# A fused five-stage kernel: inverse norms from Ln and Exp with a Newton step, band masks from half arrays, a new order of the local attention loop

## The chip, the cores and the metric

The kernel runs on one core of a Trainium2 chip. A core has five engines that run side by side, each with a queue of its own that it works off in order: TensorE (PE, matrix products into PSUM, with weight loads listed as PEld), VectorE (DVE), ScalarE (ACT), GpSimd (POOL[...]) and SyncE (SP, which here issues the transfers). Engines wait for each other by semaphores. The metric is the device time of one execution in microseconds, as the median of some runs.

## The reference

The model has two layers of attention and feed-forward on 4 sequences of 512 tokens of width 128: a gated convolution with a scan, a mixture of experts, a global attention, and last a six-layer local attention transformer. The change lies in that last part, which is most of the time. For each layer and head (16 heads of 64):

```python
def l2norm(t):
    return t / jnp.maximum(jnp.linalg.norm(t, axis=-1, keepdims=True), 1e-12)
...
qkv = x @ Wqkv
q, k, v = jnp.split(qkv, 3, -1)
...
q = l2norm(q) * qs
k = l2norm(k) * ksc
...
q = q * cos * scale + rotate_half(q) * sin * scale
k = k * cos * inv + rotate_half(k) * sin * inv
out = local_attention(q, k, v)
...
return out @ Wo
```

`local_attention` cuts the sequence into windows of 32 queries. A window sees its own 32 keys and the 32 before them, under a band mask, with scores multiplied by 8 and a softmax. After the attention comes a feed-forward with a layer norm and an exact GELU.

## The kernel before

The residual lies transposed (features on partitions) in SBUF. The local stage is cut into chunks of 128 tokens: 6 layers x 4 sequences x 4 chunks = 96 chunks, each an object of the class `Chunk`. What one chunk does:

- `query_up(j)` (L1159) makes 512 columns of queries (j = 0, 1) or keys (j = 2, 3) in PSUM. `square(j)` (ACT, L1166) and `squares(j)` (DVE, L1195) give the squared norms of the heads, `rotate_parts(j)` (DVE, L1178 and L1182) the two products of the rotation, which `rotate_sum(j)` (POOL, L1192) adds.
- `least_norms(j)` (DVE, L1203) clamps 16 squared norms from below, and `invert_norms(j)` (POOL, L1209) raises them to the power -1/2. That is done once for the keys (`rk`) and once for the queries (`rn`). `scale` (POOL, L1221) multiplies the keys by `rk`. The queries aren't multiplied: their `rn` enters as the scale of the softmax's exponential.
- `turn_up(j)` transposes on PE (L210), and `turn_down(j)` copies the result out of PSUM (L846), on ACT or DVE as the table `COPIES` says.
- `mask` (L1291) writes the band mask into the two PSUM banks of the scores: for each half of the heads one bf16 product of the identity with a 128 x 512 table. `scores(g)` (L1303) adds 128 small products, 64 rows by 32 columns of the array each.
- `largest` (DVE, L1315), `bias` (DVE, L1321) and `exponentials(g)` (ACT, L1331, 4 heads a call) make the softmax, `invert` (DVE, L1339) and `divide` (POOL, L1343) its division. `flip_up`/`flip_down` transpose the weights, `weigh` (L1379) multiplies them with the values, `lift` copies out, `output` (L1403) projects, and `add` (DVE, L1411) adds to the residual.
- `value`/`keep` (L1237, ACT L1243) make the values, and `spread` (SP, L1252 to L1257) copies them into the layout of the windows by 8 or 10 transfers a chunk.

The loop is a software pipeline. In turn i the tuple `TURN` is run through: an entry `(lag, step, ...)` runs that step of chunk i - lag. So a chunk's queries are made in one turn (lag 0), its scores in the next (lag 1), its softmax in the one after (lag 2), and so on to lag 4. The order in the tuple is the order in which each engine gets its instructions, and no engine departs from it. Turns with k = 1, 2 and 3 also take in the feed-forward of a finished sequence, a generator (`feedforward`) of which `advance` runs the next piece at the positions that `FEED` names: transposes and statistics, normalise (L202), transposes, gates with Gelu (L1431, L1436), three products (L1442), and the last product (L1452).

PSUM has two banks each for products (`mm`: query, value, projection and feed-forward products in turn) and for transposes (`tr`), and one pair each for the scores (`S`) and the weighed values (`o`). A product can start only when the bank used two products before has been read out.

The lists `MIDDLE` and `LAST` give the order by hand where the loop is filled from the global attention and where it is emptied into the last feed-forwards.

## Time and profile before

| | |
|---|---|
| Median of 3 runs | 2099.04 us (2096.14 to 2101.76) |
| The profiled execution | 2115.05 us, its span 2113.2 us |
| Mean granted TensorE clock | 0.985 |
| Global attention ends, local stage begins | at about 440 us |
| Rotation sums on POOL, L1192 | 384 x 1.275 us |
| Key scaling on POOL, L1221 | 192 x 1.043 us |
| Division on POOL, L1343 | 192 x 1.045 us |
| Exponentials on ACT, L1331 | 1536 x 0.435 us, each with a read of its sum, 0.235 us |
| Squares on ACT, L1166 | 384 x 0.633 us |
| PSUM copies 128x512, L846 | 0.59 to 0.65 us on ACT, 0.68 us on DVE |
| Normalise on DVE, L202 in the feed-forward | 88, of 0.291 at the least, 1.077 at the median |

Durations of neighbouring instructions of one engine overlap a little in the records; where a rate matters, the distance from start to start is the better measure. The profiled execution is one execution, and it took longer than the runs' median.

### The profile page before, as it was taken

Reading aid. Unit: us, or ns where it says so; the run is one execution under the profiler, and the core shown is the slowest. Engines: PE = TensorE matmul, PEld = TensorE weight load, DVE = VectorE, ACT = ScalarE, POOL = GpSimd, SP = SyncE. Lnnn points to the kernel's source line nnn. Section 1 sums busy time; section 2 is a strip of 40 time slices with the busy share of each in tenths; the row PEclk is TensorE's granted clock in tenths of the full one; section 3 lists DMA queues with packets and bytes.
Section 4 is the critical chain, followed back from the end, with each engine's and each line's share of the span. In section 5 each row is a group of like instructions: output and inputs, shape, how many; then the busy total and the mean of one; then the engine's idle time right before and its main releaser. Section 6 shows DMA issues by size and latency. Waiting matters only on the chain.

```text
span 2113.2 us, 80381 instructions
## 1 busy us (share of the span) xinstructions
PE 1980.1 (94%) x32980; PEld 1393.4 (66%) x32980; DVE 1615.3 (76%) x3343; ACT 1490.9 (71%) x4875; POOL 1722.8 (82%) x1388
## 2 busy tenths in 40 slices
PE   6778999999999999999999999999999999999997
PEld 4766777766566666666666666666666666666666
DVE  6447776687788887788877888778888788788874
ACT  2434344457788787888887788877887788877774
POOL 3425665589998899888999899998998999988882
PEclk9899999999999999999999999999999999999999
DMA  7530000002322224222232222232222322222221
GB/s 246 135 107 6 5 5 1 1 19 62 109 62 61 61 68 119 58 62 63 60 113 58 62 70 69 79 90 62 60 68 63 105 69 67 60 60 62 65 65 52
DMA packets 96665, 143.14 MB, mean 68 GB/s; under 512 B 17358, under 2 KB 41548, under 8 KB 95404
## 3 DMA queue, kind: packets, MB, share of 16 engines
q1 hardware_dynamic: 90828, 133.02, 23.3%
q8 instruction: 262, 4.29, 0.9%
q0 software_dynamic: 1472, 3.02, 0.7%
q10 hardware_dynamic: 4000, 1.97, 0.3%
q14 instruction: 103, 0.84, 0.1%
HBM read 36.36 MB, written 4.06 MB: 19 GB/s over the span
## 4 chain that ended last, share of the span: by engine, by line
PE 58%; DVE 14%; ACT 10%; issue 4%; DMA 3%; POOL 3%; SPq 2%; another core or an unknown queue 0%; ACTq 0%; DVEq 0%; POOLq 0%
PE q L1159 10%; PE lv L1237 6%; ACT lp L1331 6%; PE lo L1379 6%; PE ly L1403 5%; PE tp_r L210 5%; DMA vk<-vr 3%; PE ls L1303 3%; PE fa L1442 3%; PE fy L1452 3%; PE fg L1431 3%; PE gy L1028 2%; DVE lt L1182 2%; PE lpt L1356 2%; DVE fn L202 2%
## 5 line engine op out<-in xcount | busy, mean ns | idle before, releaser
L1331 ACT ACTIVATE lp<-ls,lnb,rn 128x64 f32<-128x64 f32 x1536 | 608.1, 435 | 32.2 <-DVE lnb L1321 31.9
L1192 POOL TENSOR_TENSOR ro<-lt,lt 128x512 f32<-128x512 f32 x384 | 484.4, 1275 | 54.2 <-DVE lt L1182 42.3
L1159 PE MATMUL q<-wqkvo,sA 128*128 128x512 f32 x768 | 383.2, 600 | 6.9 <-DVE sA L1411 4.4
L1178 DVE TENSOR_TENSOR lt<-q,rot 128x512 f32<-128x512 f32 x384 | 262.8, 684 | 148.6 <-ACT sq L1166 136.0
L1331 ACT ACTIVATION_READ_ACCUMULATOR lp<-ls,lnb,rn 128x1 f32 x1536 | 360.3, 235 | 0.0
L1209 POOL TENSOR_TENSOR rk<-rk,neg_half 128x16 f32<-128x16 f32 x96 | 279.0, 2906 | 52.3 <-DVE rk L1203 52.2
L1209 POOL TENSOR_TENSOR rn<-rn,neg_half 128x16 f32<-128x16 f32 x96 | 277.9, 2895 | 24.5 <-DVE rn L1203 22.0
L1166 ACT ACTIVATE sq<-q 128x512 f32<-128x512 f32 x384 | 235.3, 633 | 48.1 <-PE q L1159 28.7
L210 PEld LDWEIGHTS tp_r<-ident,ro 128*128 128x128 f32 x1536 | 183.6, 141 | 118.3 <-issue 94.5
L1182 DVE TENSOR_TENSOR lt<-q,rot 128x512 f32<-128x512 f32 x384 | 260.8, 679 | 0.0
L1195 DVE TENSOR_REDUCE ss<-sq 128x8 f32<-128x512 f32 x384 | 251.2, 674 | 2.3 <-ACT sq L1166 2.2
L1237 PE MATMUL lv<-wqkvo,sA 128*128 128x512 f32 x384 | 210.3, 630 | 23.2 <-DVE lt L1182 20.6
L1379 PE MATMUL lo<-lpT,vk 64*64 64x32 f32 x12288 | 206.0, 220 | 20.8 <-issue 19.6
L1243 ACT COPY vr<-lv 128x512 f32<-128x512 f32 x192 | 118.6, 618 | 151.2 <-PE lv L1237 98.7
L1379 PEld LDWEIGHTS lo<-lpT,vk 64*64 64x64 f32 x12288 | 192.3, 135 | 39.9 <-issue 37.9
L210 PE MATMUL tp_r<-ident,ro 128*128 128x128 f32 x1536 | 216.7, 274 | 1.6 <-ACT lpT L846 0.7
L1343 POOL TENSOR_TENSOR lp<-lp,lsum 128x512 f32<-128x512 f32 x192 | 196.5, 1045 | 9.7 <-DVE lsum L1339 9.7
L1221 POOL TENSOR_TENSOR ro<-ro,rk 128x512 f32<-128x512 f32 x192 | 196.2, 1043 | 7.4
L1159 PEld LDWEIGHTS q<-wqkvo,sA 128*128 128x128 f32 x768 | 128.7, 191 | 107.7 <-issue 45.4
L1403 PEld LDWEIGHTS ly<-oT,wqkvo 128*128 128x128 f32 x1536 | 182.2, 193 | 11.4 <-issue 10.6
L1403 PE MATMUL ly<-oT,wqkvo 128*128 128x128 f32 x1536 | 188.9, 277 | 0.3 <-ACT oT L846 0.3
L1303 PEld LDWEIGHTS ls<-kT,qT 64*32 64x32 f32 x12288 | 141.0, 105 | 43.4 <-issue 20.6
(305 smaller groups left out, 3628.8 us busy)
## 6 DMA issues: line engine op xcount, KB each, us to landing
vk<-vr SPq DMA_DIRECT2D x576, 128.0 KB
vk<-vr SPq DMA_DIRECT2D x336, 64.0 KB
wqkvo<-in_lwqkv_dram SPq DMA_DIRECT2D x6, 1536.0 KB
w<-in_ew_dram SPq DMA_DIRECT2D x20, 322.0 KB
wqkvo<-in_lwo_dram SPq DMA_DIRECT2D x6, 512.0 KB
ew<-in_ew_dram SPq DMA_DIRECT2D x8, 322.0 KB
ew<-in_ew_dram SPq DMA_DIRECT2D x8, 256.0 KB
lw<-in_lw_dram SPq DMA_DIRECT2D x6, 341.0 KB
```

What stands on the lines that cost most here:

```text
L210: nc.tensor.transpose(tp[:, c * P : (c + 1) * P], i[:, c, :], ident)
L1159: nc.tensor.matmul(q, lhsT=self.xs, rhs=self.w["qkv"][:, j * 512 : (j + 1) * 512], start=True, stop=True,)
L1166: nc.scalar.activation(self.sq[j], self.q[j], AF.Square)
L1178: nc.vector.tensor_tensor(heads(t1), heads(q), cs[:, None, :].to_broadcast([P, 8, DH]), ALU.mult)
L1182: nc.vector.tensor_tensor(swapped(t2), swapped(q)[:, :, ::-1, :], sn[:, None].to_broadcast([P, 8, 2, 32]), ALU.mult,)
L1192: nc.gpsimd.tensor_tensor(self.rot[j], *self.parts.pop(j), ALU.add)
L1195: nc.vector.tensor_reduce(self.ss[:, j * 8 : j * 8 + 8], heads(self.sq[j]), AX.X, ALU.add)
L1209: nc.gpsimd.tensor_tensor(self.r[j], self.r[j], neg_half.to_broadcast([P, HEADS]), ALU.pow)
L1237: nc.tensor.matmul(v, lhsT=self.xs, rhs=self.w["qkv"][:, (4 + j) * 512 : (5 + j) * 512], start=True, stop=True,)
L1331: nc.scalar.activation(self.P[:, i, :], self.S[:, i % 2, i // 2 * KB : (i // 2 + 1) * KB], AF.Exp, bias=self.nb[:, i : i + 1], scale=self. ...
L1379: nc.tensor.matmul(self.o[to : to + DH, odd, t0 : t0 + QB], lhsT=vk[r][lo : lo + KB, s, :], rhs=self.pT[lo : lo + KB, s, r * QB : (r + 1) ...
L1403: nc.tensor.matmul(y, lhsT=self.w["o"][:, j, :], rhs=self.oT[:, j % 2, j // 2, :], start=j == 0, stop=j == INNER // P - 1,)
```

## The change

It has four parts. The inverse norm is no longer a power on POOL. One clamp on DVE takes all 32 squared norms (queries and keys) and multiplies them by -1/2. ACT takes Ln and Exp of that for a first value y, and POOL makes one Newton step on y in four operations. At the start of the global attention and after each Gelu, the table set that holds both Ln and Exp is loaded ahead. `bias` goes from DVE to POOL. The band mask is no longer a product over 128 rows: the masks repeat every 32 queries, so 64 rows hold all that is needed, and the two products of a chunk use the upper and the lower 64 rows of the array, with a table `row_of` in place of the identity. Last, `TURN`, `COPIES` and `FEED` are new, with steps split finer. `MIDDLE` no longer holds three steps (`ru0.2`, `di1.0`, `ru3.2`), which now fall into the loop, and `LAST` begins with four steps more (`roa0 li0.0 di1.1 roa3`), since the loop hands over in another state.

```diff
+LOG_EXP = "natural_log_exp_and_others"
...
-NM = 2 * M_BAND + T
+NM = 2 * M_BAND + T + P
...
+    three_halves = cp.tile([P, 1], F32, name="three_halves")
+    nc.vector.memset(three_halves, 1.5)
...
+    row_of = mask_h[:, 2 * M_BAND + T :]
...
         def least_norms(self, j):
 
-            name = ("rn", "rk")[j]
-            self.r[j] = sm.tile([P, HEADS], F32, tag=name, name=f"{name}{self.tag}")
-            nc.vector.tensor_tensor(
-                self.r[j], self.ss[:, j * HEADS : (j + 1) * HEADS],
-                least.to_broadcast([P, HEADS]), ALU.max,
-            )
+            self.half_least(slice(j * HEADS, (j + 1) * HEADS), "nk"[j])
+            self.r[j] = self.x
+
+        def half_least(self, at, name):
+            x = sm.tile([P, 2 * HEADS], F32, tag="rn", name=f"r{name}{self.tag}")
+            self.x = x[:, 0 : at.stop - at.start]
+            nc.vector.tensor_scalar(self.x, self.ss[:, at], least, -0.5, ALU.max, ALU.mult)
 
         def invert_norms(self, j):
-            nc.gpsimd.tensor_tensor(
-                self.r[j], self.r[j], neg_half.to_broadcast([P, HEADS]), ALU.pow
-            )
...
+            self.inverse_root(self.r[j], "nk"[j])
+
+        def inverse_root(self, x, name):
+
+            n = x.shape[1]
+            y = sm.tile([P, 2 * HEADS], F32, tag="yn", name=f"y{name}{self.tag}", bufs=2)[:, 0:n]
+            nc.scalar.activation(y, x, AF.Ln, scale=-2.0)
+            nc.scalar.activation(y, y, AF.Exp, scale=-0.5)
+            nc.gpsimd.tensor_tensor(x, x, y, ALU.mult)
+            nc.gpsimd.tensor_tensor(x, x, y, ALU.mult)
+            nc.gpsimd.tensor_tensor(x, x, three_halves.to_broadcast([P, n]), ALU.add)
+            nc.gpsimd.tensor_tensor(x, x, y, ALU.mult)
+
+        def all_norms(self):
+
+            self.half_least(slice(0, 2 * HEADS), "qk")
+            self.r = [self.x[:, 0:HEADS], self.x[:, HEADS:]]
+
+        def invert_all(self):
+            self.inverse_root(self.x, "qk")
...
             for par in range(2):
+
+                at = slice(par * 64, par * 64 + 64)
                 nc.tensor.matmul(
-                    S[:, par], lhsT=ident_h, rhs=bands[min(self.c, 1)], start=True, stop=False
+                    S[:, par], lhsT=row_of[at], rhs=bands[min(self.c, 1)][at], start=True,
+                    stop=False,
                 )
...
+        nc.scalar.preload_act_table_set(LOG_EXP)
         yield
         for k, (f0, fn) in enumerate(DI_CH):
...
     TURN = (
-        (1, "squares", 3), (1, "rotate", 1), (1, "window"), (3, "flip", 0, "e6"),
-        (1, "values", 0), (2, "largest"), (1, "scale_keys"), (2, "bias", nc.vector),
-        (3, "flip", 1, "e7"), (2, "exponentials", 0), (1, "squares", 1), (4, "project"),
-        (2, "exponentials", 3), (1, "turn", 0, "e4"), (0, "query", 2), (1, "scale_queries"),
-        (0, "query", 0), (0, "rotate", 2), (0, "rotate", 0), (2, "exponentials", 2),
-        (1, "turn", 1, "e5"), (0, "squares", 2), (3, "weigh", 0), (3, "weigh", 1),
-        (2, "exponentials", 1), (2, "values", 1), (0, "query", 3), (1, "turn", 3, "e3"),
-        (0, "squares", 0), (1, "turn", 2, "e2"), (2, "invert", 1), (0, "query", 1),
-        (1, "mask"), (3, "lift", 1, "e1"), (2, "invert", 0), (1, "scores", 1),
-        (2, "divide", 0), (1, "scores", 0), (3, "lift", 0, "e0"), (2, "spread"),
-        (2, "divide", 1), (0, "rotate", 3),
+        (1, "rotate_sum", 0), (1, "rotate_parts", 1), (4, "lift", 0, "e0"), (3, "divide", 1),
+        (2, "largest"), (2, "bias", nc.gpsimd), (1, "rotate_sum", 1), (1, "value", 0),
+        (1, "squares", 3), (1, "keep", 0), (1, "rotate_sum", 3), (3, "flip_up", 0),
+        (3, "flip_down", 0, "e6"), (3, "flip_up", 1), (1, "window"), (1, "squares", 1),
+        (2, "exponentials", 0), (4, "output"), (4, "add"), (2, "exponentials", 1),
+        (1, "turn_up", 1), (0, "query_up", 2), (1, "turn_down", 1, "e5"), (0, "square", 2),
+        (1, "all_norms"), (3, "flip_down", 1, "e7"), (1, "invert_all"), (0, "rotate_parts", 2),
+        (0, "squares", 2), (0, "query_up", 0), (1, "scale"), (0, "square", 0),
+        (2, "exponentials", 3), (3, "weigh", 0), (3, "weigh", 1), (0, "rotate_parts", 0),
+        (2, "invert", 0), (2, "exponentials", 2), (1, "turn_up", 0), (1, "turn_down", 0, "e4"),
+        (3, "lift", 1, "e1"), (2, "value", 1), (1, "turn_up", 3), (0, "query_up", 3),
+        (0, "squares", 0), (2, "keep", 1), (2, "invert", 1), (0, "square", 3), (2, "divide", 0),
+        (1, "turn_down", 3, "e3"), (1, "turn_up", 2), (2, "spread"), (1, "mask"),
+        (0, "rotate_sum", 2), (0, "query_up", 1), (1, "turn_down", 2, "e2"), (1, "scores", 1),
+        (1, "scores", 0), (0, "rotate_parts", 3), (0, "square", 1),
     )
     COPIES = {
         "e0": "aaaa",
-        "e1": "avaa",
-        "e2": "aaaa",
-        "e3": "aaaa",
-        "e4": "avva",
-        "e5": "aavv",
-        "e6": "aavv",
-        "e7": "vavv",
+        "e1": "vavv",
+        "e2": "vvav",
+        "e3": "aava",
+        "e4": "vvaa",
+        "e5": "vvvv",
+        "e6": "vavv",
+        "e7": "vvvv",
     }
-    FEED = {1: (12, 36, 40), 2: (5, 12, 13), 3: (3, 11)}
+    FEED = {1: (7, 45, 55), 2: (10, 13, 20), 3: (17, 28)}
...
+        if i == 0:
+            nc.scalar.preload_act_table_set(LOG_EXP)
...
+    first[64:] = first[:64]
+    k, to = np.arange(P)[:, None] % 64, np.arange(P)[None, :]
+    row_of = np.where(to < QB, k == to, k == QB + to % QB)
+    m = np.concatenate([np.tile(first, (1, 8)), np.tile(band, (1, 8)), causal, row_of], 1)
```

## The prediction

> **What bounds the kernel now.** I read the page's busy shares first, then PE's timeline over one group of four chunks (a batch row of one layer), then busy time by engine over its four turns, then rows by shape. The page:
>
> ```profile
> PE 1980.1 (94%) x32980; PEld 1393.4 (66%) x32980; DVE 1615.3 (76%) x3343; ACT 1490.9 (71%) x4875; POOL 1722.8 (82%) x1388
> ```
>
> PE and POOL are both nearly full. A share can't say which one makes the others wait; the stretch by turns can (start:end, length, then busy time of each engine, the granted clock, DMA). I cut turns from one mask matmul to the next:
>
> ```profile
> 1215.32:1229.34 14.02, 14.02 (x311) 10.14 (x310) 10.16 (x21) 12.44 (x46) 13.79 (x10) 1.00 0.27 70
> 1229.34:1244.69 15.35, 14.70 (x315) 10.51 (x314) 14.20 (x33) 13.64 (x47) 15.27 (x13) 1.00 0.30 74
> 1244.69:1264.95 20.26, 19.19 (x325) 12.14 (x324) 17.38 (x31) 16.32 (x48) 17.25 (x14) 1.00 0.22 56
> 1264.95:1282.24 17.29, 17.29 (x319) 11.45 (x318) 14.45 (x27) 12.27 (x44) 15.07 (x12) 1.00 0.24 59
> ```
>
> In the first and last turn PE never stops: 14.02 us is its work for one chunk, the rest is the feed-forward laid into the turns. It loses time in the second, where POOL (fifth busy figure, 15.27 of 15.35) is full, and the third. PE's timeline there (start, duration, instruction, what it waited for):
>
> ```profile
> 1238.21 2.07 PE L1379 MATMUL lo<-lpT,vk 64*64 64x32 f32 x128
> 1240.83 1.10 PE L1237 MATMUL lv<-wqkvo,sA 128*128 128x512 f32 x2 [0.55 <-ACT lp L1331]
> 1242.03 1.10 PE L1159 MATMUL q<-wqkvo,sA 128*128 128x512 f32 x2
> ...
> 1246.70 0.55 PE L210 MATMUL tp_fb<-ident,fn 128*128 128x128 f32 x3
> 1247.88 0.33 PE L210 MATMUL tp_fb<-ident,fn 128*128 128x128 f32 x1 [0.64 <-DVE fn L202]
> 1248.05 0.60 PE L1356 MATMUL lpt<-ident,lp 128*128 128x128 f32 x4
> 1249.08 1.12 PE L1237 MATMUL lv<-wqkvo,sA 128*128 128x512 f32 x2 [0.43 <-DVE lt L1182]
> ```
>
> PE waits for DVE: for the feed-forward's normalise, and for a PSUM bank that the rotation parts empty. DVE is late because of POOL:
>
> ```profile
> 1233.03 1.13 DVE L1203 TENSOR_TENSOR rk<-ss,least 128x16 f32<-128x16 f32 x1
> 1243.76 4.07 DVE L202 TENSOR_SCALAR fn<-fn,mv_f,rs_f 128x128 f32<-128x128 f32 x4
> ```
>
> The first has a minimum of 0.155 and here takes 1.13, ending when POOL's two ro sums end (1234.1). A normalise takes 0.29 at best, 1.08 at the median, about one POOL instruction. Work of PE alone over the group: 14.02 + 14.46 (one more set of transposes, 0.44) + 18.9 (0.44 + 2.57 + 1.87 of feed-forward) + 17.29 = 64.7. Mask to mask the four turns average 67.8 over the stage (66.9 here). So PE loses 3.1 per group, and over 22 groups with a feed-forward in the table **about 68 us is the most that order and relief can give**, while PE's work stays.
>
> **The change, part by part.**
>
> *Powers on POOL.* Removed each turn:
>
> ```profile
> L1209 POOL TENSOR_TENSOR rk<-rk,neg_half 128x16 f32<-128x16 f32 x96 | 279.0, 2906 | 52.3 <-DVE rk L1203 52.2
> L1209 POOL TENSOR_TENSOR rn<-rn,neg_half 128x16 f32<-128x16 f32 x96 | 277.9, 2895 | 24.5 <-DVE rn L1203 22.0
> ```
>
> 5.80 us a turn. Added: four POOL operations on 128x32 and the bias on 128x16. POOL products on 128, 256 and 512 columns take 0.40, 0.62 and 1.04, so 1.67 ns a column on 0.18: 0.24 for 32 columns, 0.26 with some room for two full inputs (1.275 against 1.04 at 512), 0.21 for the bias. Together 1.25. POOL falls by 4.55 a turn, from 61.4 to 43 us in the group above. It ceases to bind.
>
> *Ln and Exp on ACT.* Nearest rows: 128x19 copy 0.18, 128x1 activation 0.20, 128x128 Exp 0.31. I take 0.23 each (ends 0.18 and 0.35) and 0.5 for both with the step between them. ACT loses 10 PSUM copies per group (22 "a" letters become 12) at 0.535 from start to start: 54.7 - 5.4 + 2.0 = 51 us.
>
> *Table loads.* Now a pair per feed-forward:
>
> ```profile
> L1436 ACT ACT_TABLE_LOAD x22 | 28.2, 1283 | 0.4
> L1331 ACT ACT_TABLE_LOAD x22 | 28.2, 1283 | 0.4
> ```
>
> The Trainium skill, "ScalarE: Activation LUTs", section "Table sets: the hidden batching unit", says that functions load as sets, that Exp lives in more than one, and that one set holds both Ln and Exp. The preload names that set after each Gelu, so the pair stays a pair: cost nothing. Were Ln and Exp taken from different sets, each turn would have two loads, 2 x 1.28 by the row or 2 x 2.66 by the page (which adds a drain): 2.6 to 5.3 us on ACT's busiest stretch in all 96 turns. I take nothing, and keep this as a rival.
>
> *DVE.* Ten copies come over at 0.60 from start to start, +6.0 a group; two clamps and the bias (means 0.40, 0.39, 0.26) become one clamp, -2.4. DVE goes from 56.2 to 60 us a group: the fullest engine behind PE. Cover is 4.7 us per group, not spread evenly.
>
> *Masks.* Now two 128-row bf16 products take, with the step into the scores' small tiles, 0.53 (1229.34 to 1229.87). Entering small tiles costs 0.10 (transposes 0.53 before the weighing, 0.44 before a projection), leaving them 0.10 (the value product takes 0.97 after the weighing and 0.86 elsewhere), so a mask is 0.21. On separate halves of the array the two run side by side, saving 0.21; that such halves overlap is seen in the scores, 128 products of 64 columns in 1.7 us where 64 columns at the projection's rate (0.86 per 512) would be 0.107 each, 13.7 in a row. But the masks now stand ahead of the second query product, no longer next to the scores. The Trainium skill, "TensorEngine Tiling (Array Packing)", section "Key Properties", says that changing the tiling mode drains the engine. That speaks against this part: one more entry and exit, +0.20. By the packing alone 96 turns gain 20 us; with the switches at the trace's price they gain 1. If the halves don't overlap they lose 19. I take zero.
>
> *The order table.* The chain of a turn, t = 0 at the end of the scores: maxima 0.1 to 1.3 on DVE; bias on POOL to 1.75 (before, the clamp stood between and was held until POOL finished: 1233.03 to 1234.59, 1.56, now 0.45); keep and eight exponentials (0.385 each) to 4.95; square 2 to 5.5; Ln and Exp to 6.1; four POOL steps to 7.3; key scaling 2 x 1.04 to 9.5; then transpose 3. PE without waits is at that transpose at 9.2 (value product 0.92, two flips 0.88, projection 1.79, a transpose 0.44, two query products 1.72, weighing with its entry 2.09, a transpose with the exit 0.53, value product 0.86). It waits 0.3, and the scores end near 14.3, against 14.02 before. Queued behind Ln on ACT are a square and the eight other exponentials; these end at 9.9, before the mask needs the bank at about 10.9. With a feed-forward: turn two has the normalise before the key copy on DVE. DVE gets there at 10.75 (maxima to 1.3, statistics 1.6, two reductions 1.2, add 0.6, copies 1.2, clamp 0.2, two rotation pairs 2.4, two reductions 1.2, the rest copies and a wait for the projection), POOL still has one division product and two sums; four normalises take 2.5 to 3.4, scores end at 16.3 to 16.75 (PE's own work 14.9 in this cut, with both transposes). Turn three: Gelus and loads to 5.9, exponentials, Ln at 9.8, scaling done 13.5, PE there at 13.5: 18.3. Turn four: scaling done 10.2, PE at 13: 17.5. Sum 66.4 to 66.85. Taking 66.8, **the group gains 1.0 of its 67.8**, 22 us over 22 groups. Value spreads keep their 8 or 10 transfers a chunk, 0.55 issue each; they start when the second value copy ends, 3.6 us before the turn's end (3.9 before), so SP's queue gains nothing and can cost 0.3. The lists before and after the loop move a few steps and shorten a few powers: zero.
>
> Sum: profiled span 2113.2, in an execution of 2115.1, minus 22 is 2091 and 2093. The runs' median lies 16 lower, 2099.0; minus 22 is **2077 us**.
>
> **Rivals.**
>
> *The new chain is longer than I walked (slower).* Place: the run from maxima to transpose 3, which has 0.3 us too much in turn one and nothing spare in turn three, and PE does nothing else meanwhile since its queue is in order. Each extra us costs up to two per group. It decides from 0.5 us extra, which hops or a clamp held by POOL (1.13 above) can give; with 1.2 extra the group loses 2.4 - 1.0 = 1.4, 31 us: 2130. For it: DVE, in this chain at both ends, gets fuller. Against: the 1.1 us saved ahead of the bias.
>
> *PE back to back.* If POOL, freed of a third of its work, no longer holds DVE's normalise (0.29 each, 3 us less), nearly all of the 3.1 comes back: 2099 - 63 = 2036. For it: the turns one and four of today. Against: DVE's added copies.
>
> *A wash.* Half-array masks cost their switches and the gain of turns two and three goes into turn one: 2096.
>
> *It doesn't do what it says.* Loads in every turn: 2.6 more in each chain, some 1.8 of it unhidden, 96 x 1.8: 2270.
>
> **How the numbers follow.** Main case 0.42, longer chain 0.24, back to back 0.19, wash 0.11, loads 0.04. Below 0.3% (6 us), a measurement here can't tell a change from none. Faster: 0.37 of the main case and all of back to back, 0.56 with rounding; within 0.3%: 0.05 + 0.09 + 0.02 = 0.16; slower: the rest, 0.28. The range 2028 to 2132 holds the two outer cases and leaves the loads and a worse chain out; the main case's own is 2062 to 2095.
>
> **What would show it.** Right: no powers of 2.9 us in POOL's rows; POOL near 65% of a turn; Ln and Exp at 0.2 to 0.25; 44 paired loads; normalise's mean well below 0.88. Chain: PE idle before transpose 3, released by POOL's scaling. Masks: 0.3 us from mask to query, the projection behind it 0.1 longer. Wrong: a turn without feed-forward over 14.8 us, PE waiting on DVE in every turn, or more than some 50 loads.

## The result, and the profile after

The changed kernel takes **2134.2 us** (median of 4 runs, 2125.4 to 2135.16), beside 2098.1 us (2096.14 to 2101.76) for the kernel before: a ratio of 1.0163 [1.0143, 1.0182]. It is slower by 1.6%; 2077 us and a gain were forecast.

The page of after, its head and the busy time of each engine:

```profile
span 2133.0 us, 80093 instructions
PE 1986.8 (93%) x32980; PEld 1365.6 (64%) x32980; DVE 1689.1 (79%) x3393; ACT 1410.6 (66%) x4839; POOL 1286.8 (60%) x1685
```

POOL is relieved as meant, by 436 us. The time went up nevertheless: what POOL gave up was not worth its length. The page's table of groups, for the Newton step's first product and the table loads (count, busy us, mean ns, then the idle time ahead of it and who ended it):

```profile
L1224 POOL TENSOR_TENSOR rqk<-rqk,yqk 128x32 f32<-128x32 f32 x93 | 23.5, 253 | 278.7 <-ACT yqk L1223 259.2
L1445 ACT ACT_TABLE_LOAD x22 | 28.2, 1283 | 0.4
L1448 ACT ACT_TABLE_LOAD x22 | 28.2, 1283 | 0.4
```

One of the step's four operations takes 0.25 us, where each of the two powers took 2.9, and the loads are still 22 pairs. But POOL now stands idle for 259 us in front of that product, waiting for ACT's Exp. POOL's spare time has become waiting time for a chain that runs through ACT.

The four turns of one group, from mask to mask, for after (start:end, length, busy time of PE, PEld, DVE, ACT and POOL, clock, DMA):

```profile
1217.54:1231.92 14.38, 14.17 (x313) 9.77 (x312) 13.14 (x24) 10.84 (x43) 10.30 (x15) 1.00 0.30 73
1231.92:1247.19 15.27, 14.59 (x315) 10.28 (x315) 14.70 (x32) 12.29 (x46) 11.55 (x16) 1.00 0.28 70
1247.19:1267.57 20.38, 19.65 (x326) 12.09 (x326) 16.46 (x30) 16.50 (x50) 10.47 (x15) 1.00 0.22 54
1267.57:1284.85 17.28, 17.28 (x320) 11.21 (x320) 14.29 (x25) 11.44 (x44) 10.80 (x15) 1.00 0.25 61
```

The first turn now holds a wait of PE that it did not have. The third, where most was to be won, is as long as before. The group shown is a good one; over 20 groups (layers two to six, counted at the projections) the mean is 69.23 us, before 68.00. By turn, from mask to mask, these 20 groups take 14.40, 15.89, 20.49 and 18.33 after and 14.10, 15.96, 20.40 and 17.37 before: turn three stays, and what is lost lies in turns one and four, though turn four of the group shown has no part in it. From the first query product to the end the local stage takes 1724.5 us after and 1686.1 before, 38.4 more: 24.6 in these 20 groups, 5.0 in the two groups ahead of them, 2.9 in the lists by hand before and 5.9 in the list behind. (The spans differ by only 20 because the profiled execution of before took 19 us longer in the stages ahead, which are the same in both.)

PE's timeline over part of turn one and the start of turn two (start, duration, instruction, what it waited for):

```profile
1228.80 1.02 PE L1247 MATMUL lv<-wqkvo,sA 128*128 128x512 f32 x2
1230.03 0.66 PE L216 MATMUL tp_r<-ident,ro 128*128 128x128 f32 x4 [0.21 <-POOL ro L1240]
1230.52 1.02 PE L1165 MATMUL q<-wqkvo,sA 128*128 128x512 f32 x2
1231.38 0.60 PE L216 MATMUL tp_r<-ident,ro 128*128 128x128 f32 x4
1231.92 0.39 PE L1303 MATMUL ls<-mask_h 64*128 64x512 bf16 x2
1232.23 1.13 PE L1165 MATMUL q<-wqkvo,sA 128*128 128x512 f32 x2
1233.29 1.60 PE L1316 MATMUL ls<-kT,qT 64*32 64x64 f32 x128
```

It shows two things. Transpose 3 (the first `tp_r` here) waits for POOL's key scaling (before, such waits were PE's on DVE). And the mask pair takes 0.31 from start to start, where I had figured 0.21; the query product behind it takes 1.06 to the scores, not 0.86: two changes of tile, of 0.10 each.

PE's timeline in turn three of after, around the projection:

```profile
1254.98 1.02 PE L1452 MATMUL fa<-xn,lw 128*128 128x512 f32 x2
1255.84 0.60 PE L1369 MATMUL lpt<-ident,lp 128*128 128x128 f32 x4
1256.91 2.05 PE L1410 MATMUL ly<-oT,wqkvo 128*128 128x128 f32 x16 [0.47 <-DVE fh L1455]
```

and ACT's timeline behind it:

```profile
1254.22 1.83 ACT L1445 ACTIVATE fh<-fg,vec 128x512 f32<-128x512 f32 x3
1256.07 1.28 ACT L1448 ACT_TABLE_LOAD   x1
...
1261.22 0.60 ACT L1172 ACTIVATE sq<-q 128x512 f32<-128x512 f32 x1 [0.65 <-PE q L1165]
1261.71 0.22 ACT L1222 ACTIVATE yqk<-rqk 128x32 f32<-128x32 f32 x1
```

The feed-forward's product `fa` now stands ahead of the projection. The projection needs a PSUM bank that DVE's multiply by the Gelu must release, and the Gelus end at 1256.05. PE starts 0.47 us late, so the query product is late, ACT waits 0.65 for it with its square, and Ln stands behind that square. A wait of PE comes back as a later Ln, later scaled keys and a second wait of PE (0.26 at transpose 3 of this turn). All projections of a run in one row (the idle time ahead of them behind the second bar), before and then after:

```profile
L1403 PE MATMUL ly<-oT,wqkvo 128*128 128x128 f32 x1536 | 188.9, 277 | 0.3 <-ACT oT L846 0.3
```

```profile
L1410 PE MATMUL ly<-oT,wqkvo 128*128 128x128 f32 x1536 | 192.6, 279 | 22.4 <-DVE fh L1455 11.6
L1410 PEld LDWEIGHTS ly<-oT,wqkvo 128*128 128x128 f32 x1536 | 180.3, 193 | 44.7 <-ACT vr L1253 25.6
```

Half of PE's new wait (11.6) ends with DVE's multiply by the Gelu, in turn three. Most of the other half (9.9) ends with ACT's copy of a value product, in turn four; the weight loads (PEld) wait mostly for that copy.

### The profile page after: what moved, and what is told of

It is laid out like the page before. It is cut to its first block, busy times and chain, and to the rows that moved or that the text cites. A ratio compares the mean times of both kernels' runs of the same rounds, so it can differ in the third digit from the quotient of the medians.

```text
span 2133.0 us, 80093 instructions
## 1 busy us (share of the span) xinstructions
PE 1986.8 (93%) x32980; PEld 1365.6 (64%) x32980; DVE 1689.1 (79%) x3393; ACT 1410.6 (66%) x4839; POOL 1286.8 (60%) x1685
## 4 chain that ended last, share of the span: by engine, by line
PE 58%; ACT 12%; POOL 12%; DVE 9%; issue 4%; DMA 3%; SPq 0%; ACTq 0%; DVEq 0%; POOLq 0%
PE q L1165 11%; PE tp_r L216 6%; POOL ro L1240 6%; PE ly L1410 6%; ACT lp L1344 6%; PE ls L1316 4%; PE lv L1247 4%; PE lo L1392 3%; PE fy L1462 3%; PE gy L1034 2%; PE fg L1440 2%; ACT sq L1172 2%; DMA vk<-vr 2%; PE fa L1452 2%; PE gs L956 2%
## 5 line engine op out<-in xcount | busy, mean ns | idle before, releaser
L1344 ACT ACTIVATE lp<-ls,lnb,rqk 128x64 f32<-128x64 f32 x1488 | 579.0, 415 | 15.1 <-POOL lnb L1334 14.8
L1165 PE MATMUL q<-wqkvo,sA 128*128 128x512 f32 x768 | 393.7, 609 | 3.1 <-DVE sA L1418 1.4
L1172 ACT ACTIVATE sq<-q 128x512 f32<-128x512 f32 x384 | 229.2, 597 | 208.4 <-PE q L1165 194.3
L1344 ACT ACTIVATION_READ_ACCUMULATOR lp<-ls,lnb,rqk 128x1 f32 x1488 | 320.1, 215 | 0.0
L216 PE MATMUL tp_r<-ident,ro 128*128 128x128 f32 x1536 | 241.8, 281 | 34.2 <-POOL ro L1240 21.9
L1201 DVE TENSOR_REDUCE ss<-sq 128x8 f32<-128x512 f32 x384 | 257.2, 675 | 2.8 <-ACT sq L1172 2.2
L1410 PE MATMUL ly<-oT,wqkvo 128*128 128x128 f32 x1536 | 192.6, 279 | 22.4 <-DVE fh L1455 11.6
L1240 POOL TENSOR_TENSOR ro<-ro,rqk 128x512 f32<-128x512 f32 x186 | 190.1, 1043 | 7.3
L1224 POOL TENSOR_TENSOR rqk<-rqk,yqk 128x32 f32<-128x32 f32 x93 | 23.5, 253 | 278.7 <-ACT yqk L1223 259.2
L1165 PEld LDWEIGHTS q<-wqkvo,sA 128*128 128x128 f32 x768 | 122.5, 190 | 72.1 <-ACT sq L1172 21.9
L1316 PE MATMUL ls<-kT,qT 64*32 64x64 f32 x12288 | 158.1, 227 | 1.4 <-issue 1.4
```

Of the source, the lines that this page charges most:

```text
L216: nc.tensor.transpose(tp[:, c * P : (c + 1) * P], i[:, c, :], ident)
L1165: nc.tensor.matmul(q, lhsT=self.xs, rhs=self.w["qkv"][:, j * 512 : (j + 1) * 512], start=True, stop=True,)
L1172: nc.scalar.activation(self.sq[j], self.q[j], AF.Square)
L1240: nc.gpsimd.tensor_tensor(k, k, self.r[1][:, j * 8 : j * 8 + 8, None].to_broadcast([P, 8, DH]), ALU.mult,)
L1316: nc.tensor.matmul(S[to : to + QB, par, s, :], lhsT=self.qT[lo : lo + 64, s, to : to + QB], rhs=self.kT[lo : lo + 64, s, to : to + KB], st ...
L1344: nc.scalar.activation(self.P[:, i, :], self.S[:, i % 2, i // 2 * KB : (i // 2 + 1) * KB], AF.Exp, bias=self.nb[:, i : i + 1], scale=self. ...
```

## The experiments

All ratios are to the kernel before on the same chip. That kernel's median there is 2096 to 2118 us. The group is the mean of 20, as above, from one profiled execution. e13 and e16 have the same loop, and their groups differ by 0.17; smaller differences of a group mean nothing, nor do some 3 us in the sums over 20 groups below.

| run | ratio | 95% | group, us |
|---|---|---|---|
| before | 1 | | 68.00 |
| after | 1.0163 | 1.0143 to 1.0182 | 69.23 |
| e1_norms_in_old_order | 1.0109 | 1.0085 to 1.0133 | 68.77 |
| e9_norms_and_copies_in_old_order | 1.0043 | 1.0026 to 1.0059 | 68.15 |
| e2_masks_in_old_order | 0.9996 | 0.9983 to 1.0008 | 68.07 |
| e3_old_masks_in_new_order | 1.0130 | 1.0111 to 1.0149 | 68.59 |
| e7_masks_beside_scores | 1.0161 | 1.0130 to 1.0192 | 69.28 |
| e4_norms_before_exponentials | 1.0360 | 1.0334 to 1.0387 | 71.40 |
| e6_old_copies_in_new_order | 1.0402 | 1.0370 to 1.0434 | 71.51 |
| e5_key_scales_swapped | 1.0155 | 1.0126 to 1.0184 | 69.06 |
| e8_swapped_and_old_masks | 1.0137 | 1.0103 to 1.0171 | 69.33 |
| e10_feed_positions_2_3 | 1.0066 | 1.0040 to 1.0093 | 68.61 |
| e11_normalise_earlier | 1.0128 | 1.0111 to 1.0145 | 68.79 |
| e12_feed_positions_1_2_3 | 1.0030 | 1.0018 to 1.0042 | 68.20 |
| e13_best_order_masks_beside | 1.0001 | 0.9989 to 1.0013 | 67.72 |
| e15_best_order_old_masks | 1.0000 | 0.9987 to 1.0014 | 67.97 |
| e14_best_order_powers | 1.1135 | 1.1110 to 1.1161 | 78.22 |
| e16_tail_norms_first | 0.9994 | 0.9983 to 1.0004 | 67.55 |
| e17_tail_positions | 1.0012 | 0.9995 to 1.0028 | 67.85 |

For the comparison of orders I added up, from PE's records, what lies between the start of one block of matmuls and the start of the next beyond the block's own work, in us over 20 groups. Changes of tile and waits inside a block are included. The order before has other neighbours, and a pair that does not occur there is marked -. Its own largest sums, not in the table, are 30.0 from weighing to value, 14 to 15 from the feed-forward's transposes to a flip, and 12 each from value to query and from flip to value.

| from -> to | before | after | e4 | e6 | e5 | e10 | e11 | e12 |
|---|---|---|---|---|---|---|---|---|
| value -> transpose 3 | - | 24.0 | 1.2 | 53.2 | 2.8 | 4.6 | 3.9 | 5.0 |
| flip -> projection | 0.3 | 18.8 | 20.1 | 18.9 | 18.6 | 4.7 | 19.7 | 5.9 |
| feed-forward product -> projection | - | 9.9 | 9.5 | 7.1 | 16.6 | 0 | 15.9 | 0 |
| feed-forward transposes -> scores | - | 8.4 | 15.1 | 9.1 | 21.3 | 22.6 | 1.9 | 1.9 |
| query -> weighing | - | 9.7 | 37.1 | 11.1 | 9.7 | 18.4 | 9.6 | 16.7 |
| weighing -> transpose | - | 14.0 | 21.1 | 22.5 | 14.9 | 17.6 | 17.2 | 17.9 |
| transpose -> query | 0.9 | 4.5 | 26.6 | 4.4 | 1.5 | 1.3 | 4.8 | 5.7 |
| all places | 109.6 | 134.1 | 177.6 | 179.8 | 130.7 | 121.8 | 125.4 | 113.6 |

The loss of after over 20 groups, 24.5 us, is all in this sum, since PE's own work did not change (1250.3 us before, 1250.4 after). In the rows query -> weighing and weighing -> transpose some 8 us each are no waits but the change of tile, 0.10 in each of 80 turns.

### One part alone, in the old order

**e1_norms_in_old_order**: the kernel before with the new norms (clamp, Ln, Exp, Newton step, loads ahead), for keys and queries each where its power stood.

```diff
         def invert_norms(self, j):
-            nc.gpsimd.tensor_tensor(
-                self.r[j], self.r[j], neg_half.to_broadcast([P, HEADS]), ALU.pow
-            )
+            self.inverse_root(self.r[j], "nk"[j])
```

> The kernel before with the norms from Ln, Exp and the Newton step alone: old order, old copies, old masks, bias on DVE. Two clamps, two Ln/Exp pairs and eight small POOL operations a turn in place of two powers. If the loss of the change is in its order (Ln and Exp behind eight exponentials on ACT, ten more copies on DVE), this one is faster than before: POOL falls by 5.8 - 8 x 0.23 = 4.0 us a turn, and the 15 us for the normalise and part of the 30 us for the product after the weighing come back: 2060 to 2090 us. If Ln and Exp on ACT are what costs, in whatever place, it is slower than before: 2110 to 2140. POOL busy falls from 1723 to about 1350 in both.

It is slower by 1.1% with 372 us less on POOL (1350.6 busy, 1722.8 before). The waits view between 620 and 1990 us (who, for whom: us in total, times, longest), before:

```profile
DVE lt L1178 <- ACT sq L1166: 106.2, 118, 2.5
...
POOL rk L1209 <- DVE rk L1203: 43.6, 38, 2.0
...
ACT vr L1243 <- DMA vk<-vr: 38.0, 37, 2.8
```

and of this run:

```profile
POOL rk L1222 <- ACT yk L1221: 175.7, 76, 5.9
...
DVE lt L1182 <- ACT yn L1220: 83.8, 60, 1.8
...
ACT vr L1265 <- DMA vk<-vr: 78.8, 60, 3.7
...
DVE lt L1182 <- ACT sq L1170: 41.6, 59, 1.3
```

For the keys POOL waits for ACT's Exp four times as long as it waited for DVE's clamp. DVE's rotation waits 125.4 for ACT (83.8 and 41.6; 106.2 before) and ACT's value copies twice as long for the transfers: ACT's queue has become the chain. PE pays in two places: from transpose to query 20.6 us over 20 groups (0.9 before) and from query to mask 21.7 (0.6 before). The feed-forward's transposes ahead of a flip give back 14 (15.2 to 1.1), the gain that I had forecast; the 30.0 from weighing to value stay (31.9).

**e9_norms_and_copies_in_old_order**: e1, with six more of a group's PSUM copies on DVE, so that ACT has room.

```diff
-        "e4": "avva",
-        "e5": "aavv",
-        "e6": "aavv",
+        "e4": "vvvv",
+        "e5": "vvvv",
+        "e6": "vvvv",
```

> The kernel before with the new norms (as in the run e1) and six of each 32 PSUM copies moved from ACT to DVE: those between the exponentials. e1 lost 40 us per 80 turns where PE waits for the mask's bank and for a product's bank, both held by a fuller ACT, and won 23 where POOL had held DVE. Theory that Ln and Exp cost by filling ACT's queue: the copies taken out (3.2 us a group) about pay for the four small activations (4 us), the 40 shrink to under 15 and the 23 stay: ratio 0.990 to 1.000. Theory that it is Ln's wait for DVE in ACT's queue, not the sum of ACT's work: no gain against e1, 1.009 to 1.015.

Of 1.1% of loss 0.4% remains. The wait from transpose to query falls from 20.6 to 4.9; the one from query to mask (19.8) stays. That is between my two forecasts. ACT's load is a cause of e1's loss, and by these waits the larger one.

**e2_masks_in_old_order**: the kernel before with the masks from half arrays; **e3_old_masks_in_new_order**: after with the masks over 128 rows; **e7_masks_beside_scores**: after with the step `mask` right ahead of the scores.

```diff
-                    S[:, par], lhsT=ident_h, rhs=bands[min(self.c, 1)], start=True, stop=False
+                    S[:, par], lhsT=row_of[at], rhs=bands[min(self.c, 1)][at], start=True,
+                    stop=False,
```

(e2; e3 is the reverse in after.)

```diff
-        (1, "turn_down", 3, "e3"), (1, "turn_up", 2), (2, "spread"), (1, "mask"),
-        (0, "rotate_sum", 2), (0, "query_up", 1), (1, "turn_down", 2, "e2"), (1, "scores", 1),
+        (1, "turn_down", 3, "e3"), (1, "turn_up", 2), (2, "spread"),
+        (0, "rotate_sum", 2), (0, "query_up", 1), (1, "turn_down", 2, "e2"), (1, "mask"), (1, "scores", 1),
```

> The kernel before with the half-array masks alone, which there stand right before the scores. In the changed kernel a mask pair takes 0.32 us (not 0.43) and two mode switches more of 0.10. Here there is no switch between masks and scores if the 64-row mask counts as the scores' mode: 0.10 us saved a turn, 10 us in 96 turns: 2088. If every change of tile shape drains, the step from 64x128 to 64x32 costs 0.1 as well, and the time stays at 2096 to 2100.

> The changed kernel with 128-row masks in the same place in the order. If the two switches more cost what the trace of the changed kernel shows, 0.085 us a turn net of the shorter pair, this gains 8 us: 2126. If the half-array masks pay, it loses up to 10 us: 2144. The theory of the long chain has no part in it.

> The changed kernel with the half-array masks moved behind the query product, right before the scores. In the old order that place had no switch between masks and scores and a net of nothing against the 128-row masks. Here it takes away one switch into small tiles and one out, 0.2 us a turn, 19 us in 96 turns if nothing else holds PE then: ratio 1.007 to 1.009. If the scores wait for the key copy of transpose 2 anyway (8 us in 80 turns ahead of the scores in one turn of four), a part stays: 1.010 to 1.013.

In the old order the part is worth nothing; PE's timeline of e2:

```profile
1228.06 0.39 PE L1293 MATMUL ls<-mask_h 64*128 64x512 bf16 x2
1228.38 1.77 PE L1306 MATMUL ls<-kT,qT 64*32 64x64 f32 x128
```

The pair takes 0.32 to the scores with no further step; two 128-row products with the step took 0.53. But a step of 0.10 now comes ahead of the masks: over 20 groups the sum gains 8.8 at the masks and 7.6 behind them and pays 8.1 ahead, which the group does not show (68.07 against 68.00): small waits in other places take it back. So the time came out as I had forecast for a further step of 0.10 between masks and scores, and there is none. In after the masks stand apart from the scores, so the array changes its tiles twice more: 7.7 ahead of the masks and 11.8 behind the query product (5.5 there with the old masks), against 8.9 won. With the old masks after's group is 0.64 us shorter, 12.8 over 20; 5.1 of that is this sum, the rest are waits that went with it (6 of them ahead of the projection behind a feed-forward product). By the medians the gain is 0.3%, and the two intervals overlap a little. Moving the masks beside the scores (e7) gains nothing in after, where I had forecast 0.3% at the least: 5.8 and 17.5 go to waits ahead of them, behind a query product and behind the feed-forward's transposes. The entry 55 of `FEED` stayed where it was in e7 and so came to stand behind the copy of transpose 2; e13 below moves it along. In the mended order below it gains.

### The chain to the keys

**e4_norms_before_exponentials**: after, with the clamp, Ln and Exp ahead of the eight first exponentials. The feed-forward's positions are counted in steps, so positions 17 and 20 (turns three and four) shift by two steps against the rest as well.

```diff
-        (2, "exponentials", 0), (4, "output"), (4, "add"), (2, "exponentials", 1),
+        (1, "all_norms"), (2, "exponentials", 0), (1, "invert_all"), (4, "output"), (4, "add"), (2, "exponentials", 1),
...
-        (1, "all_norms"), (3, "flip_down", 1, "e7"), (1, "invert_all"), (0, "rotate_parts", 2),
+        (3, "flip_down", 1, "e7"), (0, "rotate_parts", 2),
```

> The changed kernel with the clamp right after the second of the two reductions and Ln, Exp and the POOL steps queued after the first four exponentials, ahead of the next four and of a square. Theory of the chain: transpose 3 waits for scaled keys in every turn (24 us in 80 turns), and this brings the scaling forward by 1.5 to 2.0 us, so the wait goes: 24 to 28 us, 2106 to 2110. Theory of DVE's load (ten copies more, all of them late in the turn): the wait only moves to another place, 2125 to 2135.

The wait for the keys goes, from 24.0 to 1.2, and the group is 2.2 us longer than after's: both forecasts are missed. PE now waits ahead of the weighing (37.1) and of a query product (26.6). The clamp itself, by tile, in after (duration min/median/max in ns) and below it in this run:

```profile
L1213 DVE TENSOR_SCALAR rqk<-ss,least x93: 229/241/272, 465.2 to 2059.1; 128x32 f32<-128x32 f32 x93
```

```profile
L1213 DVE TENSOR_SCALAR rqk<-ss,least x93: 241/978/1223, 478.4 to 2119.1; 128x32 f32<-128x32 f32 x93
```

In its new place, beside POOL's 512-column operations, it takes four times as long (one at 1187.89 ends at 1188.87, when two of POOL's rotation sums end at 1188.83). With two positions shifted at once, the run says that this earlier place of Ln is no cure, not how much of its cost is the clamp's.

**e5_key_scales_swapped**: after, with the key scaling of the half that transpose 3 needs first; **e8_swapped_and_old_masks**: the same with the old masks.

```diff
-            for j in range(2):
+            for j in (1, 0):
                 k = heads(self.rot[2 + j])
```

> The changed kernel with the two key scalings on POOL in the other order: the half that transpose 3 needs first. No other engine's queue changes. Theory of the late keys: transpose 3 waits 0.3 to 0.47 us a turn for the second scaling of 1.04, the wait goes (24 us in 80 turns, some 28 in all): ratio to before 1.003 to 1.006. Theory that DVE's fuller queue is what costs: PE gets to the next wait sooner and waits there, as in the run with early norms: less than 8 us gained, ratio 1.012 to 1.016.

> Key scalings swapped and 128-row masks in the new order. If late keys (28 us) and mask switches (7 us by the timing, 13 by the local stage of the trace) are separate costs, they add: 0.999 to 1.003, as fast as before. If they cover each other, 1.005 to 1.010.

The wait at transpose 3 falls by 21.2, the sum of all by only 3.4: the waits from the feed-forward's transposes to the scores (8.4 to 21.3) and ahead of the projection (9.9 to 16.6) take its place. PE's timeline of e5 shows the next in line, a transpose of the feed-forward that waits for its normalise:

```profile
1230.00 0.58 PE L216 MATMUL tp_fb<-ident,fn 128*128 128x128 f32 x2 [0.75 <-DVE fn L208]
```

e8's ratio lies 0.2% under e5's, and the intervals overlap; its group is no shorter. Even the worse of my two forecasts (1.010) was too good. Why the old masks gained 0.6 us of a group in e3 and nothing here stays open.

**e6_old_copies_in_new_order**: after with the old table of copies, so 10 of a group's copies go back from DVE to ACT.

```diff
     COPIES = {
         "e0": "aaaa",
-        "e1": "vavv",
-        "e2": "vvav",
-        "e3": "aava",
-        "e4": "vvaa",
-        "e5": "vvvv",
-        "e6": "vavv",
-        "e7": "vvvv",
+        "e1": "avaa",
+        "e2": "aaaa",
+        "e3": "aaaa",
+        "e4": "avva",
+        "e5": "aavv",
+        "e6": "aavv",
+        "e7": "vavv",
     }
```

> The changed kernel with the PSUM copies shared out as before (10 of each 32 back from DVE to ACT, DVE 6.0 us a group less, ACT 5.4 more). If DVE's load is the cause, the waits for rotation parts, key copies and the feed-forward's products shrink: 10 to 25 us faster than the changed kernel, ratio 1.004 to 1.011. If the exponentials' chain on ACT is the cause, ten copies more on ACT make it longer: ratio 1.02 to 1.04.

It costs 2.4% more. The wait for the keys doubles (53.2). So taking DVE's added copies back, which I held to be the danger, is no cure: ACT's queue ahead of Ln is the more sensitive place. That DVE's load costs nothing doesn't follow, since ACT got it at the same time.

**e14_best_order_powers**: the mended order of e12 (below) with one power of 32 columns on POOL in place of Ln, Exp and the Newton step (the clamp then no longer multiplies by -1/2).

```diff
-            nc.scalar.activation(y, x, AF.Ln, scale=-2.0)
-            nc.scalar.activation(y, y, AF.Exp, scale=-0.5)
-            nc.gpsimd.tensor_tensor(x, x, y, ALU.mult)
-            nc.gpsimd.tensor_tensor(x, x, y, ALU.mult)
-            nc.gpsimd.tensor_tensor(x, x, three_halves.to_broadcast([P, n]), ALU.add)
-            nc.gpsimd.tensor_tensor(x, x, y, ALU.mult)
+            nc.gpsimd.tensor_tensor(x, x, neg_half.to_broadcast([P, x.shape[1]]), ALU.pow)
```

> The run e12 with the inverse norm as one power on POOL over 32 columns, no Ln, no Exp, no Newton step. By the rows of before (2.90 for 16 columns, 1.02 for 4) a power on 32 takes some 5.4 us against 0.5 for Ln and Exp and 1.3 for four POOL steps. If the new norms are what makes this order possible, keys are late in every turn by 2 to 3 us: ratio 1.05 to 1.12. If POOL's relief gave nothing in the new order either, it stays within 1% of e12.

11% slower. The group on POOL (busy us, mean ns), and PE's waits of this run:

```profile
L1220 POOL TENSOR_TENSOR rqk<-rqk,neg_half 128x32 f32<-128x32 f32 x93 | 504.6, 5426 | 167.0 <-DVE rqk L1213 164.4
```

```profile
PEld tp_r L216 <- POOL ro L1233: 279.4, 165, 3.6
...
PE tp_r L216 <- POOL ro L1233: 178.0, 73, 2.8
```

One power of 5.43 us between clamp and scaling is more than this order has time for, where the order before, with its earlier powers of 2.9, gave each its place. The new order needs the new norms, or at least no power of 32 columns in that place; the old one loses by them (e1).

### The feed-forward's positions

Three runs on top of e5, in which only the places of the feed-forward's pieces change:

```diff
-    FEED = {1: (7, 45, 55), 2: (10, 13, 20), 3: (17, 28)}
+    FEED = {1: (7, 45, 55), 2: (10, 20, 21), 3: (7, 28)}
```

for **e10_feed_positions_2_3** (no product of the feed-forward between a Gelu or a value product and the projection),

```diff
+    FEED = {1: (7, 27, 55), 2: (10, 13, 20), 3: (17, 28)}
```

for **e11_normalise_earlier**, and for **e12_feed_positions_1_2_3** both:

```diff
+    FEED = {1: (7, 27, 55), 2: (10, 20, 21), 3: (7, 28)}
```

> The changed kernel with swapped key scalings, and the feed-forward's products at other positions in turns three and four: the first and second a-product behind the projection, the third ahead of the value product, so that the projection no longer needs a bank that a Gelu or the first value copy has just to release. PE waits 29 us in 80 turns there. Theory that these waits are separate costs of the new positions: 20 to 30 us off, ratio 1.002 to 1.006. Theory that DVE, full from the normalise to the next maxima, sets the pace and PE's waits only move: under 8 us, 1.011 to 1.016.

> The changed kernel with swapped key scalings, and the normalise of the feed-forward in turn two moved on DVE from position 45 (between reductions late in the turn, beside POOL operations of 1.0 to 1.27 us, 3.15 to 3.4 us in all) to 27 (beside POOL's idle time and its four short steps). If the late normalise makes DVE the pace of turns two and three, it takes under 2.2 us there, the key copy is early and the wait ahead of the scores (21 us in 80 turns after the swap) goes: ratio 1.004 to 1.008. If the exponentials' chain on ACT sets the pace, the same wait shows up behind the squares: 1.012 to 1.018.

> Both moves at once. If positions in the table are what the change lost by, and they are separate, it is as fast as before: 0.992 to 1.000. If PE's waits move from place to place since ACT's chain (maxima, bias, exponentials, value copy, value transfers, next value copy) is a loop longer than PE's work, it stays over 1.008.

This is where most can be won back. From 1.0155 (e5), e10 comes to 1.0066, e11 to 1.0128, e12 to 1.0030, 1.25% together. The waits ahead of the projection (18.6 and 16.6 in e5) fall to 4.7 and 0 by e10, and the row of all projections has next to no idle time left:

```profile
L1410 PE MATMUL ly<-oT,wqkvo 128*128 128x128 f32 x1536 | 188.0, 276 | 0.5 <-ACT oT L852 0.5
```

e11 takes the waits from the feed-forward's transposes to the scores from 21.3 to 1.9, as forecast, though its ratio is the one forecast for no cure; e12 lies between its two forecasts. The normalise by tile in after and then in e12:

```profile
L208 DVE TENSOR_SCALAR fn<-fn,mv_f,rs_f x88: 330/544/1416, 552.1 to 2008.2; 128x128 f32<-128x128 f32 x88
```

```profile
L208 DVE TENSOR_SCALAR fn<-fn,mv_f,rs_f x88: 330/336/397, 541.1 to 1972.8; 128x128 f32<-128x128 f32 x88
```

At position 27 POOL waits for Ln and Exp or does the short operations of the Newton step, and DVE is free of it: 0.34 each against 1.08 in the kernel before. In after 60 of the 88 still run beside a POOL operation of over 0.6 us (1.02 in the mean, the other 28 0.33).

### The best order, and the tail

**e13_best_order_masks_beside**: e12 with the masks beside the scores (as e7, with the entry 55 of `FEED` moved along to 54). **e15_best_order_old_masks**: e12 with the masks over 128 rows. **e16_tail_norms_first**: e13, and in the list `LAST` the key norms of the last chunk ahead of the exponentials. **e17_tail_positions**: e16, with the last feed-forward's pieces later in the last turns.

```diff
-roa0 li0.0 di1.1 roa3 v1.2 v1.3 mx.2 vc1.2 vc1.3 nb.2 tu0 fl0.1 tc0 ly.0 sq3 nk fl1.1 fc0.1 tfA
-la.0 fc1.1 ex2.2 we0.1 ex3.2 ex0.2 ex1.2 ro1 in1.2 we1.1 pk in0.2 v0.3 cfA sk tu2 roa1 sq1 mask win
+roa0 li0.0 di1.1 roa3 v1.2 v1.3 mx.2 vc1.2 vc1.3 nb.2 tu0 fl0.1 tc0 ly.0 sq3 nk pk fl1.1 fc0.1 tfA
+la.0 fc1.1 ex2.2 we0.1 ex3.2 ex0.2 ex1.2 ro1 in1.2 we1.1 in0.2 v0.3 cfA sk tu2 roa1 sq1 mask win
```

(e16), and for e17 also

```diff
-            slots += {3: (20, 34), 0: (5, 40)}.get(k, ())
+            slots += {3: (20, 48), 0: (5, 58)}.get(k, ())
```

> The run e12 (swapped scalings, three feed positions moved) with the half-array masks right before the scores. In e12 entering and leaving small tiles around the mask still costs PE 10.6 us in 80 turns net of the shorter pair. Theory that PE is now near its own pace: most of it comes back, 8 to 12 us, ratio 0.997 to 0.999. Theory that the exponentials' chain still sets the pace, as when the same move gained nothing in e7: the scores wait for the exponentials' bank or the maxima are no earlier, 1.002 to 1.004.

> The run e12 with 128-row masks in the same place, which have no switch into and out of the 64-row mode ahead of the query product. By the changed kernel's trace and e3 the half-array masks in that place cost 0.09 us a turn: 8 us, ratio 0.998 to 1.000. If the pace is set by the exponentials, no gain: 1.002 to 1.004.

> The run e13 with one more move, in the list that empties the loop: Ln, Exp and the Newton step for the last chunk's keys queued ahead of the previous chunk's sixteen exponentials instead of behind them. In the changed kernel's trace PE stands 3.4 us there for the scaled keys, and the stretch behind the loop is 3 to 6 us longer than before. If Ln behind exponentials is the price of the new norms here as well, 3 us: ratio 0.998 to 0.999, at the edge of what can be told. If the weighing and the projections behind it wait anyway, none.

> e16 with the extra feed positions of the last layer, which the change left at numbers that belong to the old table (20, 34 and 5, 40 of 42 entries), moved to like places of the new one (20, 48 and 5, 58 of 60). They act on two sequences only; PE has single waits of 2 to 2.5 us there. If the numbers were simply stale, 2 to 4 us over e16: 0.996 to 0.998. If the waits are DVE's, none or a loss of 1 to 2 us.

e13, e15 and e16 take as long as the kernel before (1.0001, 1.0000, 0.9994, each with 1 in its interval), e13 between its two forecasts; e17's positions gain nothing. In e13 PE's sum is 103.9 over 20 groups against 109.6 before, which is the 0.28 us by which its group is shorter. Half-array masks beside the scores and full masks come out the same here (e13 and e15), and half-array masks ahead of the query product 0.3% worse (e12). The whole change is worth nothing measurable, once its order is mended. In the tail, after has a wait that the list caused (PE's timeline):

```profile
2082.46 1.12 PE L216 MATMUL tp_r<-ident,ro 128*128 128x128 f32 x4 [3.38 <-POOL ro L1240]
```

`LAST` had the key norms' power on POOL behind the exponentials, where it cost ACT nothing. Now the same place puts Ln behind sixteen exponentials in ACT's queue. With the step moved forward (e16), PE no longer waits there, and the part behind the last full group takes 129.8 us (133.2 in e13, 136.0 in after, 130.1 before).

## Why the prediction was wrong

**What bounds the kernel** was read in the right places: PE's waits are what changed from run to run. That POOL holds up DVE is right too: the normalise went from 1.08 to 0.34 where POOL is quiet (e12). What it is worth was over-read: PE's waits for DVE went, and others came.

**The single terms** nearly all fit: POOL's busy time of a group 43 us (43.1), ACT 51 (51.1), DVE 60 (58.6); Ln and Exp 0.23 each (0.23, 0.23); the Newton steps 0.24 to 0.26 (0.24 to 0.25); the bias 0.21 (0.22); 44 paired loads; the four normalises 2.5 to 3.4 (3.15 in turn two of the group shown). The Trainium skill, "ScalarE: Activation LUTs", section "Table sets: the hidden batching unit", was right that one set holds both Ln and Exp, as the 44 loads show (none stands between Ln and Exp), and the rival of loads in every turn is out. The 2.66 us that the prediction took from that page for a load with its drain are not seen: from the end of the operation ahead of a load to the start of the one behind it 1.31 us pass.

**The signs** mostly came as listed for a right prediction, and none of those for a wrong one did: a turn without feed-forward takes 14.40, nearly all of PE's waits on DVE lie in turn three, and there are 49 loads in all. They did not watch the places where it failed. One for "right" did fail: the normalise's mean fell from 0.86 only to 0.80, since at its new position 45 most of them still run beside POOL's long operations.

**The masks** were mis-sized: a pair takes 0.31 to 0.32, not 0.21. By the records both products of a pair start together (0.22 apart before), yet the next block starts as late as if they overlapped by half. A pair of 0.21 and a step of 0.10 would look the same; against it speaks that the query product behind, with its 1.06, already holds both steps. So the sign "0.3 us from mask to query" came true by a longer pair. The changes of tile cost 0.10 each way, as I took from the trace, and as the Trainium skill, "TensorEngine Tiling (Array Packing)", section "Key Properties", warned in kind: it says that changing the tiling mode drains the engine. Instead of the 0 taken, the part loses 5.1 over 20 groups in its place, and perhaps 0.3% with what follows from it (e3, not seen in e8).

**The step that failed is the walk of the order table, above all its turns three and four.** From the end of one turn's scores to the end of the next, as it was walked, over 20 groups:

| turn | walked | measured |
|---|---|---|
| one | 14.3 | 14.46 |
| two | 16.3 to 16.75 | 16.74 |
| three | 18.3 | 19.60 |
| four | 17.5 | 18.30 |

Turns one and two are right. In turn three I followed the chain from maxima to transpose 3 ("exponentials, Ln at 9.8, scaling done 13.5, PE there at 13.5") and let PE run up to it without a stop: the 18.3 is no more than PE's own work of that turn by my own figures (18.9, less the 0.44 of transposes that this cut counts in turn two). I left out what PE's own queue had to wait for on that way: the feed-forward products that the new `FEED` puts ahead of the projection, so that the projection needs a bank that a Gelu (turn three) or a value copy (turn four) must first release. Ahead of it lie 13.9 us in turn three and 9.9 in turn four over 20 groups, 1.2 us a group. e10 moves these products alone and gets 0.9% back. That PE's lateness comes back over the square ahead of Ln was missing as well: transpose 3 waits 9.3 for its keys in turn three and 7.1 in turn two, where the walk had only 0.3 a group, in turn one. The four turns come to 69.1 instead of 66.8, and 2.3 us over 22 groups are 51 of the 57 us by which the forecast is off.

**"The lists before and after the loop … zero"** is the second error: 2.9 and 5.9 us. I counted the powers that they shorten, and not that they move the work into a queue with exponentials in it (e16).

**The rival of a longer chain** gave 2130 us and 24 in a hundred, close to the measured time, but its mechanism holds only in part. PE does wait for the scaled keys, 24.0 us over 20 groups, 1.2 a group. That wait does not decide: swapping the key scales takes 21 of the 24 away and gains 3.4, since other waits take its place. So the closeness of its number is luck in part. **Back to back** did not come: of PE's waits those for the normalise go, but with 372 us less on POOL e1 is slower, by the chain through ACT.

**Left open.** What is left between weighing and the next transpose beyond the change of tile, 6 to 15 us over 20 groups in the runs of the new order; what the copies' wait for the value transfers costs, which grows as the order is mended (49.1 us in a whole run before, 57.4 in after, 98.5 in e13) and which no run took away; and the old masks in e8.

## What to carry to other kernels

A relief of the fullest engine is worth what the new place of the work leaves of it: here 436 us of POOL's time went, and two short activations in ACT's in-order queue cost more than they saved in the old order (e1). In the new one the change came out even only when the key scalings, the feed-forward's positions and the place of the masks were mended. When an order table is placed anew, walk PE's own queue too: for each product, who releases the bank it needs, and whether that hangs on a slow activation or a transfer. Undoing one wait gains its own length only if the next one stands well behind it; so look at the sum of all waits, not at the one that the trace names first.

## What was not expected of the hardware

- A DVE tensor_scalar from SBUF to SBUF takes 0.24 or 0.98 us (the clamp in after and e4), and 0.34 or 1.08 (the normalise in e12 and before), by what POOL does meanwhile. The work is the same. All 93 clamps of after have no POOL operation of over 0.6 us beside them and take 0.23 to 0.27; in e4 69 have one and take 1.03 in the mean.
- Two 512-column bf16 products on separate 64-row halves of the array take 0.31 to 0.32 us as a pair, three quarters of the 0.43 that two over all rows take (0.53 less the step of 0.10). From these half-array tiles to the scores' 64 by 32 tiles no step is seen (0.32 as well, in e2), if the pair's own time is read as above.
- POOL's power costs by the column: 1.01 us for 128x4 columns, 2.90 for 16, 5.43 for 32, while a product of 32 columns there takes 0.25.
